# A PSUM bank that keeps operands: y terms, convolution sums and router scratch move in, the third bank for short results goes

## The chip, the cores and the metric

The kernel runs on one core of one Trainium2 chip. The metric is the device time in microseconds of one execution, as the median of several runs. The engines are named as in the profile: PE (TensorE matmuls), PEld (its weight loads), DVE (VectorE), ACT (ScalarE), POOL (GpSimd) and SP (SyncE, which issues most DMAs).

## The reference

Input `x` is 8 images of 256 channels by 32 x 32 pixels, float32. Three layers follow each other, each with a residual. Cut to what matters:

```python
# layer 0: deformable attention on group-normalised x (4 groups = heads of 64 channels)
q   = gconv1x1(x, wq)                                   # 1024 queries per image
off = tanh(pw(gelu(depthwise_conv6x6_stride4(q)))) * 4  # 64 sample places per group
kv  = grid_sample(x, grid + off); k, v = gconv1x1(kv, wk), gconv1x1(kv, wv)
pos = grid_q - grid_kv                                  # 1024 x 64 pairs, x and y
bias = sign(pos) * log1p(abs(pos))
bias = relu(bias @ w1.T + b1)                           # 2 -> 64
bias = relu(bias @ w2.T + b2)                           # 64 -> 64
bias = bias @ w3.T + b3                                 # 64 -> 1
x = x + wo(softmax(q*scale @ k.T + bias) @ v)
# layer 1: tokens t (1024 x 256 per image), n = layernorm(t)
t = t + sigmoid((n @ qw) @ n.T) @ n
# layer 2: mixture of experts, 8 experts, the best 2 per token, n = layernorm(t)
t = t + n + sum over the 2 experts of weight * (gelu(n @ w1[e] + b1[e]) @ w2[e] + b2[e])
```

The position bias of layer 0 is the bulk of the work: 8 x 4 x 1024 x 64 pairs go through a small network of widths 2, 64, 64 and 1.

## The kernel before, in words

**Turns.** The position network sets the beat. An image (a "batch", `b`) takes 128 steps in 64 turns of two steps; the loop over `n` at the end of `tile_conv_attn_hybrid` writes out one turn after the other, and the order in which instructions are written is the order on each engine (`in_order` fixes it). The first layer of a step is separable: a term `ta` that depends on x and a term `nb` that depends on y. An even step computes `ta - nb` on POOL (L465) and ACT rectifies it (L470). An odd step, the "second form", computes `max(ta, nb)` on DVE (L463), and what that leaves out is put right by a term `nc` that `second` gets from `nb` by a small matmul `cp` (L446, copied by ACT in L451). The second layer is the matmul group `h2p` (L478) on PE into one of two tiles of two banks, which ACT empties for even steps (L484) and DVE for odd ones (L486). The third layer is `sim` (L505), every second turn. First-layer results are made two turns ahead (four steps in flight, six buffers).

**Tables.** Every eight turns `terms` loads the next `ta` and `nb`; `scale` (turn 3 of 8) scales them on ACT and DVE (L440), `second` (turn 4 of 8) makes `nc`, and from turn 6 the new table is in use.

**What is laid between the turns.** Each turn takes one step of several generators: `prep` for the next image (group norm, queries, the 36 taps of the convolution on DVE in L284 and L286, three a turn, Gelu, sampling weights, `tp` transposes in L374, `kv`, `kp`), `softmax` (transposes `lt` and `at_`, product `ov`), `attention` of the image before (`upper` and `rest`, with `slots`, `finish` and then `route`), `experts` of an older image (`yp` L921, `hp` L939, `tp` L957), and `combine` (POOL gathers in L992, DVE sums in L984, `op` in L975).

**PSUM.** There are eight banks: one for `sim`, four for `h2p`, two that rotate for short results (`psum(name)`), and one more (`acc(name)`). `aside(name)` takes the bank of `acc`, except while `attending` is set, when it takes one of the two rotating ones:

```python
    def aside(name):
        return psum(name) if attending else acc(name)
```

In `slots`, step `n` makes the scores `ap` of one slot (L713), ACT takes the sigmoid `sg` (L718), and PE adds the product of the slot before to `vp` (L727). `vp` lies in `acc`'s bank and collects all slots of a quarter `q` of the queries (two or four), and then DVE adds it to `x1` (L733). `route` takes `acc`'s bank for the transposed router scores and as scratch for DVE. The convolution's sums `oc` lie in SBUF. The flag `attending` also steers how the last image's experts are laid in.

Of the kernel before, what the change touches and what calls it, by code (L numbers as in the profile page):

```python
# [16 lines left out]
P = 128  # L17
# [5 lines left out]
E = 8  # L23
# [80 lines left out]
def tile_conv_attn_hybrid(ctx: ExitStack, tc: tile.TileContext, x, par, qw, w1, w2_, cst, out):  # L104
# [6 lines left out]
    t8 = ctx.enter_context(tc.tile_pool(name="t8", bufs=7))  # L111
    t2 = ctx.enter_context(tc.tile_pool(name="t2", bufs=11))
    hpool = ctx.enter_context(tc.tile_pool(name="h", bufs=1))
# [20 lines left out]

    def acc(name):
        return ps_a.tile([P, 512], F32, tag="acc", name=name)


    attending = sorting = False

    def aside(name):
        return psum(name) if attending else acc(name)

# [93 lines left out]
    def prep(b, xb, st):  # L237
# [3 lines left out]
        for k in range(2):  # L241
# [3 lines left out]
            yield  # L245
        gm = aside("gm")
        nc.tensor.matmul(gm[:, 0:2], lhsT=cst_("gavg"), rhs=mv[:, :, 0], start=True, stop=True)
# [6 lines left out]
        yield  # L254
        gv = aside("gv")
        nc.tensor.matmul(gv[:, 0:2], lhsT=cst_("gavg"), rhs=dm, start=True, stop=True)
# [12 lines left out]
        for k in range(2):  # L269
            for h in range(2):  # L270
                qs = (aside if h else psum)("qs")
                nc.tensor.matmul(qs, lhsT=wq[:, k, :], rhs=xn[:, k, halves(h)], start=True, stop=True)
                nc.scalar.copy(inside(qp, k, h), qs.rearrange("p (r f x) -> p r f x", f=4, x=W))
            yield


        oc = one.tile([P, 16, 8], F32, name="oc")
        dw = par_("dw")
        for t in range(KS * KS):
# [7 lines left out]
            if t % 3 == 2:  # L287
                yield
        nc.scalar.activation(oc, oc, AF.Gelu)
        oa = oc.rearrange("p (y k) x -> p k y x", k=2)  # L290
        yield


        op = aside("op")
        for g in range(2):
# [33 lines left out]

        fp = aside("fp")  # L330
        nc.tensor.transpose(fp[:, 0:128], ft, ident)
# [33 lines left out]
        for t in range(0, 10, 2):  # L365
            if t:
                w2_ = wt[:, t - 2 : t, :]
                nc.gpsimd.tensor_tensor(w2_, w2_, hx.unsqueeze(1).to_broadcast([P, 2, 256]), ALU.mult)
            if t < 8:
                tp = aside("tp")  # L370
# [12 lines left out]
        kv = aside("kv")  # L383
        for k in range(2):
# [13 lines left out]
        yield  # L398
        kp = aside("kp")
        for k in range(2):  # L400
# [23 lines left out]
    def terms(b, k, h, part):  # L424
# [29 lines left out]

        return (ta, nb, nc_, b, number), scale, second

    def first_layer(terms_, n):
        ta, nb, nc_, of, number = terms_
        h1 = hpool.tile([P, 2, 16, W], F32, name="h1", bufs=6)
        a = ta[:, n].unsqueeze(2).to_broadcast([P, 2, 16, W])  # L460
        b = nb[:, n].unsqueeze(3).to_broadcast([P, 2, 16, W])
        if second_form(of, number, n):
            nc.vector.tensor_tensor(h1, a, b, ALU.max)  # L463
            return h1, nc_[:, :, n // 2]
        nc.gpsimd.tensor_tensor(h1, a, b, ALU.subtract)  # L465
        return h1, None
# [127 lines left out]
    def attention(b, st, o, rt):  # L594
        nonlocal attending
        x = xres.pop(b)
# [106 lines left out]
        def slots(todo, last):  # L703
            sg = None
            for n in range(len(todo) + 1):
                sg_, sg = sg, None
                if n < len(todo):
                    q, mp = todo[n]
                    ap = psum("ap").rearrange("p (u i) -> p u i", u=2)
                    for u in range(2):  # L710
                        m0 = (2 * mp + u) * P
                        for k in range(2):
                            nc.tensor.matmul(  # L713
                                ap[:, u, :], lhsT=tn[:, k, m0 : m0 + P], rhs=qt[:, k, quarter(q)],
                                start=(k == 0), stop=(k == 1),
                            )
                    sg = low("sg")
                    nc.scalar.activation(sg, ap, AF.Sigmoid)  # L718
                if sg_ is not None:
                    q, mp = todo[n - 1]  # L720
                    first = n == 1 or todo[n - 2][0] != q
                    end = n == len(todo) or todo[n][0] != q
                    if first:
                        vp = acc("vp").rearrange("p (i c) -> p i c", i=2)
                    for u in range(2):
                        for i in range(2):
                            nc.tensor.matmul(  # L727
                                vp[:, i, :], lhsT=sg_[:, u, i * P : (i + 1) * P], rhs=tt[:, 2 * mp + u, :],
                                start=(first and u == 0 and i == 0), stop=(end and u == 1), skip_group_check=True,
                            )  # L730
                    if end:
                        xs = x1[:, 2 * q : 2 * q + 2, :]
                        nc.vector.tensor_tensor(xs, xs, vp, ALU.add)  # L733
                        if last:
                            finishing.append(finish(q))
                yield
# [55 lines left out]
    def route(lqs, rt, slots_):  # L792
# [5 lines left out]

        revv = rev.unsqueeze(1).to_broadcast([P, 8, E])
        bank = acc("lp")  # L800

        def part(n, size=64):
            a = bank[:, Q + 64 * n : Q + 64 * n + size]
            return a.rearrange("p (m e) -> p m e", e=E) if size == 64 else a

        for c in range(2):
            nc.tensor.transpose(bank[:, c * P : (c + 1) * P], lqs[:, c * P : (c + 1) * P], ident)
# [37 lines left out]
        most = N // slots_  # L845
        need = bank[:, Q + 64 : Q + 64 + 8 * most].rearrange("p (e n) -> p e n", e=E)
        nc.vector.tensor_tensor(
# [8 lines left out]
        nc.vector.tensor_reduce(ends[:, 1:9], part(1), AX.X, ALU.add)  # L856
        for c in range(2):
            nc.vector.tensor_scalar(ws[c], m1, 0.5 - c, 0.5, ALU.mult, ALU.add)
        yield
        at = part(3)  # L860
        nc.vector.scalar_tensor_tensor(
            at, ends[:, 0:8].unsqueeze(1).to_broadcast([P, 8, E]), float(slots_), cnt[:, 0:8, :], ALU.mult, ALU.add
        )
        place = one.tile([P, 2, 8], F32, name="place")
        for c, oh in enumerate((oh1, oh2)):
# [4 lines left out]
        yield  # L870
        which = bank[:, 0 : TILES * (E - 1)].rearrange("p (t e) -> p t e", e=E - 1)
        nc.vector.tensor_tensor(
# [13 lines left out]
    def experts(b, rt):  # L886
# [28 lines left out]
        for n in range(rounds + 2):  # L915
# [107 lines left out]
    total = NB * STEPS  # L1023
    table, scale, second = terms(0, 0, 0, 0)
# [28 lines left out]

# [26 lines left out]
    for n in range(NB * TURNS):  # L1080
# [16 lines left out]
        if coming_ < total and n % 8 == 0:  # L1097
            b_, k_, h_ = place(coming_)
            coming, scale, second = terms(b_, k_, h_, coming_ // 16 % 2)
        if n % 8 == 6 and coming_ < total:  # L1100
# [150 lines left out]
```

## Time and profile before

| | us |
|---|---|
| runs (3): median, lowest, highest | 3148.32, 3146.1, 3148.73 |
| the profiled execution, its own time | 3125.55 |
| its span, first to last instruction | 3123.8 |
| PE busy | 2832.1 (91% of the span) |
| DVE busy | 2170.5 (69%) |
| ACT busy | 1824.4 (58%) |
| POOL busy | 1558.2 (50%) |
| mean granted TensorE clock | 0.975 |

Busy times come from one profiled execution. A group of the profile is a line of the kernel with an engine, an operation and the tiles it writes and reads (`out<-in`); behind the bar stand the busy time in all and the mean of one in ns, and behind the second bar the idle time of the engine just before these instructions with what ended it. Idle time of an engine that nobody waits for costs nothing.

### The profile page before, as it was taken

The numbers are of one execution on the slowest core, as the hardware profiler recorded it, in microseconds if no ns is written. First come the engines' busy times: TensorE is split into PE (matmuls) and PEld (weight loads), VectorE is DVE, ScalarE is ACT, GpSimd is POOL, SyncE is SP. The second block draws the span as 40 slices with busy tenths as digits, with TensorE's granted clock in tenths as the row PEclk, the third lists the DMA queues.
The fourth block names the chain that finished last, engine by engine and source line by source line (L and its number), as shares of the span: only waits on it lengthen the run. The fifth ranks groups of instructions, "written<-read, shape, count | busy, mean of one in ns | idle before, by whom it ended". The sixth has DMA issues, their size and how long they took to land. (4 is left out here: it accounts for less than half of the span.)

```text
span 3123.8 us, 51635 instructions
## 1 busy us (share of the span) xinstructions
PE 2832.1 (91%) x19592; PEld 1395.6 (45%) x19592; DVE 2170.5 (69%) x2999; ACT 1824.4 (58%) x2533; POOL 1558.2 (50%) x945
## 2 busy tenths in 40 slices
PE   3888998899999999999999999899999999979975
PEld 2223343233545344453545445354444545514764
DVE  4897678967776687857876678766877574595122
ACT  3666565665576566665566656665666666554322
POOL 2546454744455364645556455553646443383122
PEclk7999999999999999999999999999999999989998
DMA  3312101211256125531346223561245325631386
GB/s 106 83 32 48 21 14 32 58 38 21 75 139 187 23 63 140 168 107 43 77 111 208 51 57 100 144 179 33 61 132 173 88 78 153 173 97 57 112 280 221
DMA packets 428297, 311.21 MB, mean 100 GB/s; under 512 B 284432, under 2 KB 368656, under 8 KB 428048
## 3 DMA queue, kind: packets, MB, share of 16 engines
q1 hardware_dynamic: 415472, 273.14, 32.7%
q0 software_dynamic: 12288, 33.57, 3.4%
q8 instruction: 154, 2.52, 0.3%
q10 hardware_dynamic: 288, 1.20, 0.1%
q14 instruction: 95, 0.78, 0.1%
HBM read 239.93 MB, written 67.90 MB: 99 GB/s over the span
## 5 line engine op out<-in xcount | busy, mean ns | idle before, releaser
L465 POOL TENSOR_TENSOR h<-ta,nb 128x1024 f32<-128x1024 f32 x512 | 1071.6, 2095 | 1036.2 <-PE h2p L478 913.1
L478 PE MATMUL h2p<-h,pr__100 64*64 64x512 f32 x8192 | 1028.3, 610 | 131.8 <-DVE h L486 107.5
L486 DVE TENSOR_TENSOR h<-h2p,nc 128x1024 f32<-128x1024 f32 x512 | 624.6, 1220 | 461.4 <-PE h2p L478 454.7
L484 ACT ACTIVATE h<-h2p,pr__100 128x1024 f32<-128x1024 f32 x512 | 570.9, 1115 | 517.0 <-PE h2p L478 515.8
L463 DVE TENSOR_TENSOR h<-ta,nb 128x1024 f32<-128x1024 f32 x512 | 769.2, 1503 | 0.3
L470 ACT ACTIVATE h<-h 128x1024 f32<-128x1024 f32 x512 | 538.0, 1051 | 63.4 <-POOL h L465 63.2
L478 PEld LDWEIGHTS h2p<-h,pr__100 64*64 64x64 f32 x8192 | 253.7, 133 | 658.0 <-issue 295.1
L505 PE MATMUL sim<-h,pr__100 128*32 128x512 f32 x4096 | 511.5, 618 | 0.0
L505 PEld LDWEIGHTS sim<-h,pr__100 128*32 128x32 f32 x4096 | 109.5, 112 | 377.8 <-issue 377.8
L713 PE MATMUL ap<-qt,tn 128*128 128x256 f32 x1024 | 250.5, 388 | 0.5 <-ACT nc L451 0.5
L727 PE MATMUL vp<-tt,sg 128*128 128x256 f32 x1024 | 243.3, 381 | 0.3 <-ACT sg L718 0.3
L992 POOL DMA_INDIRECT gs<-ys,slot x128 | 139.0, 1086 | 175.3 <-DMA ys<-yt 55.7
L713 PEld LDWEIGHTS ap<-qt,tn 128*128 128x128 f32 x1024 | 185.2, 190 | 88.5 <-issue 55.0
L947 ACT ACTIVATE ht<-hp,w 128x128 f32<-128x128 f32 (+1 forms) x366 | 108.6, 377 | 196.8 <-PE hp L939 173.2
L921 PE MATMUL yp<-w,ht 128*128 128x256 f32 x792 | 196.2, 390 | 13.7 <-DMA w<-in_w 7.0
L727 PEld LDWEIGHTS vp<-tt,sg 128*128 128x128 f32 x1024 | 193.2, 190 | 33.2 <-issue 6.9
L939 PE MATMUL hp<-xg,w 128*128 128x128 f32 (+1 forms) x1464 | 197.0, 287 | 6.7 <-ACT gk L307 2.8
L939 PEld LDWEIGHTS hp<-xg,w 128*128 128x128 f32 x1464 | 187.8, 194 | 18.3 <-ACT gk L307 3.7
L775 POOL DMA_INDIRECT xs<-ut,slot x128 | 167.8, 1311 | 51.0 <-DVE slot L869 29.4
L921 PEld LDWEIGHTS yp<-w,ht 128*128 128x128 f32 x792 | 144.4, 191 | 73.0 <-issue 34.0
L926 DVE TENSOR_TENSOR yt<-yp,w 128x512 f32<-128x512 f32 x99 | 68.3, 690 | 153.5 <-PE yp L921 127.3
L286 DVE SCALAR_TENSOR_TENSOR oc<-qp,pr__100,oc 128x128 f32<-128x128 f32 x280 | 168.9, 603 | 7.2
(266 smaller groups left out, 2468.0 us busy)
## 6 DMA issues: line engine op xcount, KB each, us to landing
w<-in_w SPq DMA_DIRECT2D x183, 384.0 KB, 3.6
w<-in_w SPq DMA_DIRECT2D x183, 257.0 KB, 3.7
ta<-fd SPq DMA_DIRECT2D x128, 256.0 KB, 5.5
xl<-xs SPq DMA_DIRECT2D x99, 256.0 KB, 3.7
ys<-yt SPq DMA_DIRECT2D x99, 256.0 KB, 2.3
nb<-fd SPq DMA_DIRECT2D x128, 128.0 KB, 5.3
xb<-in_x SPq DMA_DIRECT2D x8, 1024.0 KB, 7.2
x<-in_x SPq DMA_DIRECT2D x8, 1024.0 KB
```

The lines of the kernel that those rows point to most:

```text
L286: nc.vector.scalar_tensor_tensor(oc, tap, dw[:, t : t + 1], oc, ALU.mult, ALU.add)
L463: nc.vector.tensor_tensor(h1, a, b, ALU.max)
L465: nc.gpsimd.tensor_tensor(h1, a, b, ALU.subtract)
L470: nc.scalar.activation(h1, h1, AF.Relu)
L478: nc.tensor.matmul(h2p[gs, r, :], lhsT=par_("w2")[rs, gs], rhs=h1[rs, g].rearrange("p y x -> p (y x)"), start=True, stop=True, tile_positi ...
L484: nc.scalar.activation(h2, h2p, AF.Relu, bias=par_("cb2"))
L486: nc.vector.tensor_tensor(h2.rearrange("p r (y x) -> p r y x", x=W), h2p.rearrange("p r (y x) -> p r y x", x=W), nc_.unsqueeze(3).to_broad ...
L505: nc.tensor.matmul(sim[32 * q : 32 * q + 32, :], lhsT=par_("z3")[:, 15 - m : 47 - m], rhs=h2s[2 * u + q // 2][:, q % 2, :], start=False, s ...
L713: nc.tensor.matmul(ap[:, u, :], lhsT=tn[:, k, m0 : m0 + P], rhs=qt[:, k, quarter(q)], start=(k == 0), stop=(k == 1),)
L727: nc.tensor.matmul(vp[:, i, :], lhsT=sg_[:, u, i * P : (i + 1) * P], rhs=tt[:, 2 * mp + u, :], start=(first and u == 0 and i == 0), stop=( ...
L921: nc.tensor.matmul(yp[:, s, :], lhsT=ht[:, f, s * P : (s + 1) * P], rhs=f2[:, s * several // 2, f * C : (f + 1) * C], start=(f == 0), stop ...
L939: nc.tensor.matmul(hp[:, f, us], lhsT=f1[:, u, k * C + f * P : k * C + (f + 1) * P], rhs=xg[:, k, us], start=(k == 0), stop=(k == 1),)
```

## The change

One bank, the one that `acc` gave out, is allocated once as `still` and never rotates. Its first half, `held_nb`, holds the y terms of the eight second-form steps of the table in use; ACT copies them there in two halves (`hold(0)` behind `second`, `hold(1)` two turns later), and L463 reads its y operand from there in place of SBUF. Its other half, `shared`, holds the convolution's sums `oc` (Gelu then writes a new SBUF tile `oa`), and `route`'s scratch. All other users of `acc` and `aside` take the two rotating banks. In `slots`, `vp` sums two slots in a row, in one rotating bank, every second step, and `x1` gets its sum after each pair. The pool `t2` has 12 buffers in place of 11. In `route`, the line that reads the counts moves ahead of a `yield`. The first image's `kv` takes a tile of `h2p`.

```diff
-    t2 = ctx.enter_context(tc.tile_pool(name="t2", bufs=11))
+    t2 = ctx.enter_context(tc.tile_pool(name="t2", bufs=12))
...
-    def acc(name):
-        return ps_a.tile([P, 512], F32, tag="acc", name=name)
-    attending = sorting = False
-    def aside(name):
-        return psum(name) if attending else acc(name)
+    still = ps_a.tile([P, 512], F32, tag="still", name="still")
+    held_nb = still[:, 0:256].rearrange("p (s g y) -> p s g y", g=2, y=16)
+    shared = still[:, 256:512]
+    attending = sorting = convolving = False
...
-        gm = aside("gm")
+        gm = psum("gm")
...
-                qs = (aside if h else psum)("qs")
+                qs = psum("qs")
...
-        oc = one.tile([P, 16, 8], F32, name="oc")
+        nonlocal convolving
+        convolving = True
+        oc = shared[:, 0:128].rearrange("p (y x) -> p y x", x=8)
...
-        nc.scalar.activation(oc, oc, AF.Gelu)
-        oa = oc.rearrange("p (y k) x -> p k y x", k=2)
+        oa = one.tile([P, 2, 8, 8], F32, name="oa")
+        nc.scalar.activation(oa.rearrange("p k y x -> p y k x"), oc.rearrange("p (y k) x -> p y k x", k=2), AF.Gelu)
+        convolving = False
...
-        kv = aside("kv")
+        kv = psum("kv") if b else ps_h.tile([P, 2, 512], F32, tag="h2p", name="h2p")[:, 0, :]
...
-        kp = aside("kp")
+        kp = psum("kp")
...
+        def hold(half):
+            nc.scalar.copy(held_nb[:, 4 * half : 4 * half + 4], nb[:, 8 * half + 1 : 8 * half + 8 : 2])
...
         if second_form(of, number, n):
+            b = held_nb[:, n // 2].unsqueeze(3).to_broadcast([P, 2, 16, W])
             nc.vector.tensor_tensor(h1, a, b, ALU.max)
...
         def slots(todo, last):
-            sg = None
+            sgs = []
             for n in range(len(todo) + 1):
-                sg_, sg = sg, None
                 if n < len(todo):
                     q, mp = todo[n]
                     ap = psum("ap").rearrange("p (u i) -> p u i", u=2)
...
+                if n and n % 2 == 0:
+                    q = todo[n - 1][0]
+                    vp = psum("vp").rearrange("p (i c) -> p i c", i=2)
+                    for s in range(2):
+                        for u in range(2):
+                            for i in range(2):
+                                nc.tensor.matmul(
+                                    vp[:, i, :], lhsT=sgs[s][:, u, i * P : (i + 1) * P],
+                                    rhs=tt[:, 2 * todo[n - 2 + s][1] + u, :],
+                                    start=(s == u == i == 0), stop=(s == u == 1), skip_group_check=True,
+                                )
+                    sgs.clear()
+                if n < len(todo):
                     sg = low("sg")
                     nc.scalar.activation(sg, ap, AF.Sigmoid)
-                if sg_ is not None:
-                    q, mp = todo[n - 1]
-                    first = n == 1 or todo[n - 2][0] != q
-                    end = n == len(todo) or todo[n][0] != q
-                    if first:
-                        vp = acc("vp").rearrange("p (i c) -> p i c", i=2)
-                    for u in range(2):
-                        for i in range(2):
-                            nc.tensor.matmul(
-                                vp[:, i, :], lhsT=sg_[:, u, i * P : (i + 1) * P], rhs=tt[:, 2 * mp + u, :],
-                                start=(first and u == 0 and i == 0), stop=(end and u == 1), skip_group_check=True,
-                            )
-                    if end:
-                        xs = x1[:, 2 * q : 2 * q + 2, :]
-                        nc.vector.tensor_tensor(xs, xs, vp, ALU.add)
-                        if last:
-                            finishing.append(finish(q))
+                    sgs.append(sg)
+                if n and n % 2 == 0:
+                    xs = x1[:, 2 * q : 2 * q + 2, :]
+                    nc.vector.tensor_tensor(xs, xs, vp, ALU.add)
+                    if last and (n == len(todo) or todo[n][0] != q):
+                        finishing.append(finish(q))
                 yield
...
-        bank = acc("lp")
         def part(n, size=64):
-            a = bank[:, Q + 64 * n : Q + 64 * n + size]
+            a = shared[:, 64 * n : 64 * n + size]
...
+        bank = psum("lp")
...
-        for c in range(2):
-            nc.vector.tensor_scalar(ws[c], m1, 0.5 - c, 0.5, ALU.mult, ALU.add)
-        yield
         at = part(3)
         nc.vector.scalar_tensor_tensor(
             at, ends[:, 0:8].unsqueeze(1).to_broadcast([P, 8, E]), float(slots_), cnt[:, 0:8, :], ALU.mult, ALU.add
         )
+        yield
+        for c in range(2):
+            nc.vector.tensor_scalar(ws[c], m1, 0.5 - c, 0.5, ALU.mult, ALU.add)
...
-                tp = aside("tp").rearrange("p (k i) -> p k i", k=2)
+                tp = psum("tp").rearrange("p (k i) -> p k i", k=2)
...
     scale()
     second()
+    for half in range(2):
+        hold(half)
...
-            return softmax(sts[b], k, h, ss, os_[b], aside)
+            return softmax(sts[b], k, h, ss, os_[b], psum)
...
             elif n % 8 == 4:
                 second()
+                hold(0)
+            elif n % 8 == 6:
+                hold(1)
```

More of the change, by code (lines that the diff above doesn't have):

```diff
@@ L254, in prep @@
         yield
-        gv = aside("gv")
+        gv = psum("gv")
         nc.tensor.matmul(gv[:, 0:2], lhsT=cst_("gavg"), rhs=dm, start=True, stop=True)
@@ L288, in prep @@
                 yield
-        nc.scalar.activation(oc, oc, AF.Gelu)
-        oa = oc.rearrange("p (y k) x -> p k y x", k=2)
+        oa = one.tile([P, 2, 8, 8], F32, name="oa")
+        nc.scalar.activation(oa.rearrange("p k y x -> p y k x"), oc.rearrange("p (y k) x -> p y k x", k=2), AF.Gelu)
+        convolving = False
         yield
-        op = aside("op")
+        op = psum("op")
         for g in range(2):
@@ L328, in prep @@
         yield
-        fp = aside("fp")
+        fp = psum("fp")
         nc.tensor.transpose(fp[:, 0:128], ft, ident)
@@ L369, in prep @@
             if t < 8:
-                tp = aside("tp")
+                tp = psum("tp")
                 tpv = tp.rearrange("p (t k c) -> p t k c", k=2, c=P)
@@ L453, in second @@
                 )
-        return (ta, nb, nc_, b, number), scale, second
+        def hold(half):
+            nc.scalar.copy(held_nb[:, 4 * half : 4 * half + 4], nb[:, 8 * half + 1 : 8 * half + 8 : 2])
+        return (ta, nb, nc_, b, number), scale, second, hold
     def first_layer(terms_, n):
@@ L594, in attention @@
     def attention(b, st, o, rt):
-        nonlocal attending
         x = xres.pop(b)
@@ L799, in route @@
         revv = rev.unsqueeze(1).to_broadcast([P, 8, E])
-        bank = acc("lp")
+        assert not convolving
         def part(n, size=64):
-            a = bank[:, Q + 64 * n : Q + 64 * n + size]
+            a = shared[:, 64 * n : 64 * n + size]
             return a.rearrange("p (m e) -> p m e", e=E) if size == 64 else a
+        bank = psum("lp")
         for c in range(2):
@@ L845, in route @@
         most = N // slots_
-        need = bank[:, Q + 64 : Q + 64 + 8 * most].rearrange("p (e n) -> p e n", e=E)
+        need = shared[:, 64 : 64 + 8 * most].rearrange("p (e n) -> p e n", e=E)
         nc.vector.tensor_tensor(
@@ L870, in route @@
         yield
-        which = bank[:, 0 : TILES * (E - 1)].rearrange("p (t e) -> p t e", e=E - 1)
+        which = shared[:, 0 : TILES * (E - 1)].rearrange("p (t e) -> p t e", e=E - 1)
         nc.vector.tensor_tensor(
@@ L1023, in tile_conv_attn_hybrid @@
     total = NB * STEPS
-    table, scale, second = terms(0, 0, 0, 0)
+    table, scale, second, hold = terms(0, 0, 0, 0)
     while "sampled" not in sts[0]:
@@ L1098, in tile_conv_attn_hybrid @@
             b_, k_, h_ = place(coming_)
-            coming, scale, second = terms(b_, k_, h_, coming_ // 16 % 2)
+            coming, scale, second, hold = terms(b_, k_, h_, coming_ // 16 % 2)
         if n % 8 == 6 and coming_ < total:
```

## The prediction

> **What bounds the kernel now.** I read the page's busy times first, then the costliest groups, then the list of waits, and last the order of time around single stalls. The first line of the page gives the engine to watch:
>
> ```profile
> PE 2832.1 (91%) x19592; PEld 1395.6 (45%) x19592; DVE 2170.5 (69%) x2999; ACT 1824.4 (58%) x2533; POOL 1558.2 (50%) x945
> ```
>
> PE is idle for 3123.8 - 2832.1 = 291.7 us only, so whatever the change does must pass through that idle time or add to it. Busy time by stage (columns: stretch, its length, then PE, PEld, DVE, ACT, POOL) tells where it lies:
>
> ```profile
> 100.00:330.00 230.00, 197.53 (x1497) 57.95 (x1489) 195.32 (x229) 146.84 (x177) 126.42 (x61) 0.96 0.20 44
> 870.00:2690.00 1820.00, 1729.68 (x12273) 876.20 (x12271) 1309.66 (x1798) 1140.63 (x1610) 953.04 (x576) 1.00 0.41 111
> ```
>
> In the first batch DVE (195 of 230 us) is as loaded as PE; in the long middle, five batches of 363 us, PE is 95% busy and 90 us idle in all. The groups that the change touches, and PE's waits in front of h2p:
>
> ```profile
> L465 POOL TENSOR_TENSOR h<-ta,nb 128x1024 f32<-128x1024 f32 x512 | 1071.6, 2095 | 1036.2 <-PE h2p L478 913.1
> L478 PE MATMUL h2p<-h,pr__100 64*64 64x512 f32 x8192 | 1028.3, 610 | 131.8 <-DVE h L486 107.5
> L486 DVE TENSOR_TENSOR h<-h2p,nc 128x1024 f32<-128x1024 f32 x512 | 624.6, 1220 | 461.4 <-PE h2p L478 454.7
> ...
> L463 DVE TENSOR_TENSOR h<-ta,nb 128x1024 f32<-128x1024 f32 x512 | 769.2, 1503 | 0.3
> ...
> L286 DVE SCALAR_TENSOR_TENSOR oc<-qp,pr__100,oc 128x128 f32<-128x128 f32 x280 | 168.9, 603 | 7.2
> ```
>
> L463 and L486 have the same shape; L463 reads two SBUF tensors, L486 one PSUM tensor and one SBUF tensor. L486 lies between 1.21 and 1.23 us in all 512 rows; L463 has a median of 1.218 us, but 116 rows run to 1.4 to 4.1 us. The order of time shows what stretches them:
>
> ```profile
> 1502.79 0.97 POOL L992 DMA_INDIRECT gs<-ys,slot  x1 [0.16 <-issue]
> ...
> 1503.33 3.46 DVE L463 TENSOR_TENSOR h<-ta,nb 128x1024 f32<-128x1024 f32 x1
> ...
> 1503.78 1.92 POOL L465 TENSOR_TENSOR h<-ta,nb 128x1024 f32<-128x1024 f32 x1
> ...
> 1505.86 1.77 POOL L992 DMA_INDIRECT gs<-ys,slot  x1 [0.16 <-issue]
> ```
>
> L463 stands from 1503.33 to 1506.79: two POOL rows pass, POOL's L465 ends at 1505.70, and 1.09 us later L463 is done. The next gather (0.97 us before) takes 1.77 and ends after L463. The two engines shut each other out.
>
> **DVE gets rid of the lock.** With the y terms in PSUM, L463 has L486's operand kinds; I take 1.22 us (bounds 1.22 and today's 1.50). That frees 512 x 0.283 = 145 us of DVE. L286 becomes PSUM plus SBUF; its unlocked rows have a median of 0.446 us, L284 with the same tap takes 0.395, and L866, which reads and writes PSUM, is within 0.01 us of the SBUF-only L829 (0.232 and 0.224); I keep 0.446: 280 x 0.157 = 44 us. These 189 us count only where PE waited. So I walked through DVE's rows in time, gave a credit for each L463 row above 1.218 and L286 row above 0.446, set it to zero whenever DVE stood idle for over 0.1 us, and let each PE wait that DVE ended use up credit. Example: L463 of 2.63 us at 1245.91 gives 1.41, and 1.41 of the 1.97 us that PE waits until 1249.72 goes. In all: 17 us before 400 us, 10 to 870, 22 to 2690, 4 after: **-53**. Many waits stay: 0.44 us before h2p in turns where L486 starts at once and is simply longer than the h2p pair that covers it, and waits behind L440, L872 and L984, which stay locked. Bounds 0 and -107.5 (all of PE's waits for L486).
>
> POOL's L465 falls from 2.095 to about 1.92 us (90 us of POOL), but POOL waits for PE (913 us). It reaches PE only through ACT's L470 and L484, where PE waits 22.7 us: I take **-5** (0 to -22.7).
>
> The Trainium skill (SBUF — State Buffer, Who interferes with whom) says that DVE with two SBUF inputs and a GpSimd instruction that reads SBUF exclude each other, and that whoever starts first holds the port. The first half fits L463 against L486. The second does not fit the rows above, where L463 is shown starting 0.45 us ahead of L465 and still ends after it; by that half L465, not L463, would have been stretched there. By the first half alone the gain would be the same 53. The sum goes by the rows.
>
> **Short results get two banks where there were three.** Until now `acc` took the vp sums, lp, and outside attention also tp, lt, ov, kv and others, beside two rotating banks. Now all rotate over two, so each waits for the reader of the one two before it. No row shows that order, but before's rows give it: start of each PE group less end of the last reader of the group two earlier. The plainest place:
>
> ```profile
> 1232.54 0.66 PE L546 MATMUL lt<-cs,ss 128*128 128x128 f32 x4
> ...
> 1233.13 1.06 PE L686 MATMUL lq<-un,pr__100 128*32 128x256 f32 x8
> ...
> 1234.12 1.99 PE L921 MATMUL yp<-w,ht 128*128 128x256 f32 x8
> ...
> 1234.76 0.88 DVE L537 TENSOR_TENSOR ex<-lt,mx 128x128 f32<-128x128 f32 x4
> ```
>
> yp would take lt's bank, which DVE reads until 1235.64: PE stops for 1.52 us. A batch of the middle has nine such places: yp after lt 1.52; vp, tp and at_ right after cp (which takes both banks) 3 x 0.55; hp after prep's tp 0.48; hp after lt 1.48, of which 0.75 is a locked L463 that goes; tp after yp 1.10, and 1.44 of which 1.27 goes; hp after ov 1.70. Together 7.4 us, x 5 = 37; the first three batches have 4 and the last one, with attention alone, some 7: **+48**. High end: 82, the whole trace without any relief; low end 15, if the places that DVE empties (5.2 of the 7.4) vanish with a faster DVE. What still hides most uses is the h2p pair (1.95 us) and sim (1.92 us) between them.
>
> **Copies into the bank.** hold adds 128 ACT copies of 128x128; L451 (PSUM to SBUF, same size) has 0.365 us, so 47 us on an engine 58% busy: no cost by themselves. But the bank is one tensor, so ACT's copy, DVE's L463, the convolution and route's scratch follow each other in program order. After `second` the copy ends about 1.5 us after cp starts (cp at 1291.14, L451 done at 1292.27, plus 0.37); until then DVE's taps and the next L463 wait, and behind them that turn's evictions. In the middle PE has 3 us and more of other work and L463's result is needed two turns later: hidden. In the first two batches (16 tables, turns of 4.3 us) I count 0.4 to 0.6 us each, and 0.6 in each route: **+10** (0 to 64 x 1.6 = 100, if nothing hides it). By the skill (PSUM — Partial Sum Buffer, PSUM bank collisions raise a hardware error) two engines may not touch one bank and quadrant at once even at different columns, so the halves can't be used independently. That speaks against the change; no row of before has ACT and DVE share a bank in this way, and without this order the +10 would be 0.
>
> **Pairs in attention.** The number of vp matmuls stays. x1's adds rise from 48 to 64: 16 x 0.686 = 11 us on DVE, in its idle time. Turns become uneven: every second one loses 1.89 us of PE work that the next gets. L463, L486 and three taps are 3.8 us of DVE against a short turn of 1.95 + 1.89 us; in attention (1110 to 1245 us) L486 now ends a median of 3.4 us before PE needs its bank, so little shows: **+6** (0 to 8 batches x 8 turns x 1 us). Two copies stand before the first turn (2 x 0.365): **+1** (0 to 3). route's moved lines, the twelfth t2 buffer and Gelu's new output (0.31 us, 8 times) I put at nothing; ACT's and DVE's idle time covers them, and uncovered they are under 3 us.
>
> **Sum:** -53 - 5 + 48 + 10 + 6 + 1 = +7 us. The profiled execution took 3125.55 us (span 3123.8 and 1.75 around it), 22.8 under the median of the runs, 3148.32; the +7 applied to the median gives 3155. Its own range, with the terms half way to their bounds, is 3135 to 3180.
>
> **Rivals.** (1) Faster: DVE and ACT, freed of locks, empty the banks in time. Banks cost 20, holds and pairs nothing, POOL gives 15: -48, 3100. For it: 5.2 of 7.4 us per batch hang on DVE. Against: ov's 1.70 stems from L413's lock, which stays, and lt's 1.52 has no lock in it. It holds once the costs fall below 58 us. (2) Slower: the holds couple ACT, DVE and PE. If after each `second` PE's second h2p comes back before taps and L463 are through, 64 tables lose 0.8 us: 51 in place of 10, so 3196. DVE's margin is the start of the second h2p group less the end of the L486 one turn earlier. For this rival: the margin is 0.06 us, a bare signal's time, in half the turns before 330 us; against it: 1.1 us or more in three quarters of the middle's turns. It decides where DVE's margin is below 1 us. (3) The lock does not go: gain 0, +65, 3213; L486's 512 even rows speak against it.
>
> **How the numbers follow.** Forecast 0.47 (0.08 of it below -0.2%, 0.15 within, 0.24 above), (1) 0.27, (2) 0.20, (3) 0.04, other mishaps 0.02. 0.2% is 6.3 us, about what a measurement of this kernel can tell from no change. Faster 0.35, same 0.15, slower 0.50. The range 3100 to 3205 takes in (1) and (2).
>
> **What would show it.** L463 at 1.22 with no row above 1.3, L286 at 0.45; PE's wait for L486 before h2p near 55 us; new waits before yp, hp, tp and at_ of 40 us or more behind DVE L537, L563, L926 and ACT L451. If those stay under 20 us, (1) is right; if L463 stands idle behind ACT's copy for 50 us and PE's wait for L486 does not fall, (2).

## The result, and the profile after

The changed kernel takes 3126.21 us (median of 4 runs, 3122.98 to 3131.93) against 3148.53 (4 runs, 3146.1 to 3149.97) for the kernel before: ratio 0.9932, 95% interval 0.9913 to 0.995. It is 21 us faster, where the prediction had +7 us. The time lies in the range of the prediction; the sign was the other one.

The profiled execution of the changed kernel took 3122.98 us (span 3121.2). The spans of the two profiles shown lie 2.6 us apart only, because the profiled execution of before was a quick one. A second profile of before (span 3148.6 us) has 9.4 us more of PE's busy time and 11 us more in the last image's experts. So the profiles are compared here stage by stage, and times by the runs.

The first line of the page after:

```profile
PE 2830.1 (91%) x19592; PEld 1395.6 (45%) x19592; DVE 1979.1 (63%) x3015; ACT 1849.0 (59%) x2661; POOL 1377.1 (44%) x945
```

DVE lost 191 us of busy time and POOL 181; ACT gained 25. Idle time of PE is the same in sum (291.7 and 291.1 us; 307.1 in the second profile of before), so the stages have to be looked at one by one. Here is busy time by stage, for the first two batches of before (from the first h2p turn of a batch to that of the next):

```profile
70.80:345.20 274.40, 238.53 (x1782) 73.14 (x1781) 227.36 (x264) 175.18 (x206) 152.62 (x72) 0.96 0.24 60
345.20:680.70 335.50, 301.83 (x2102) 125.35 (x2101) 265.26 (x345) 200.85 (x250) 182.47 (x101) 0.98 0.16 36
```

and of after, then the fixed window of the middle that the prediction showed:

```profile
72.50:328.50 256.00, 231.39 (x1782) 72.36 (x1781) 203.70 (x264) 177.88 (x221) 129.60 (x71) 0.99 0.25 63
328.50:648.70 320.20, 298.92 (x2104) 124.32 (x2103) 232.34 (x347) 203.78 (x266) 155.12 (x101) 0.98 0.17 37
...
870.00:2690.00 1820.00, 1723.90 (x12170) 871.78 (x12166) 1175.10 (x1765) 1144.93 (x1674) 837.63 (x571) 0.99 0.40 110
```

The first two batches are 18.4 and 15.3 us shorter, 34 us in all. The same 1782 matmuls of the first batch keep PE busy 7.1 us less, at a clock of 0.99 in place of 0.96. In the middle PE does less in the same 1820 us (12170 matmuls where 12273 were): a batch there takes 366 us, some 3 us more than in the quick profile of before, whose tables of groups stand in the prediction, and about what its second profile has there (364 to 368). The groups after:

```profile
L484 PE MATMUL h2p<-h,pr__101 64*64 64x512 f32 x8192 | 1027.9, 610 | 97.6 <-DVE h L492 71.1 <-ACT h L490 20.9 <-issue 4.2
L471 POOL TENSOR_TENSOR h<-ta,nb 128x1024 f32<-128x1024 f32 x512 | 980.4, 1916 | 1154.9 <-PE h2p L484 991.8 <-ACT xg L966 68.3 <-issue 36.0
L492 DVE TENSOR_TENSOR h<-h2p,nc 128x1024 f32<-128x1024 f32 x512 | 625.4, 1222 | 462.3 <-PE h2p L484 455.0
L469 DVE TENSOR_TENSOR h<-ta,still 128x1024 f32<-128x1024 f32 x512 | 620.5, 1212 | 47.4 <-ACT still L458 45.4 <-ACT oa L291 0.8
L287 DVE SCALAR_TENSOR_TENSOR still<-qp,pr__101,still 128x128 f32<-128x128 f32 x280 | 126.6, 452 | 7.2
...
L458 ACT COPY still<-nb 128x128 f32<-128x128 f32 x128 | 35.2, 275 | 34.0 <-DVE h L469 33.7
```

L469 (L463 before) is down to 1.212 us, with none of its 512 rows above 1.3, L287 (L286) to 0.452, and L471 (L465) to 1.916. The lock between these two is gone: in the order of time after, L469 beside a POOL instruction keeps its length, and POOL's 2.00 us stay near their mean of 1.916:

```profile
1504.51 2.00 POOL L471 TENSOR_TENSOR h<-ta,nb 128x1024 f32<-128x1024 f32 x1 [1.54 <-PE h2p L484]
1504.65 1.22 DVE L469 TENSOR_TENSOR h<-ta,still 128x1024 f32<-128x1024 f32 x1
```

PE's wait for DVE in front of h2p fell from 107.5 to 71.1 us, and the new waits for banks are these (list of waits; us in total, times, longest):

```profile
PE hp L946 <- DVE o L569: 7.9, 5, 1.6
...
PE tp L964 <- DVE yt L933: 4.6, 11, 0.6
...
PE hp L946 <- ACT xt L377: 3.7, 10, 0.4
...
PE vp L727 <- ACT nc L453: 3.3, 7, 0.5
...
PE yp L928 <- ACT lqs L696: 2.8, 6, 0.5
```

The place that the prediction called the plainest is not among them. PE's order there, after:

```profile
1199.49 0.66 PE L552 MATMUL lt<-cs,ss 128*128 128x128 f32 x4
1200.08 1.06 PE L691 MATMUL lq<-un,pr__101 128*32 128x256 f32 x8
1201.60 1.99 PE L928 MATMUL yp<-w,ht 128*128 128x256 f32 x8 [0.47 <-ACT lqs L696]
```

yp waits 0.47 us for the reader of lq, not 1.52 us for DVE's reading of lt. In the whole trace no short result waits for lt's reader.

### The profile page after: what moved, and what is told of

Read it like the earlier page. It is cut to its first block, busy times and chain, and to the rows that moved or that the text cites. A ratio compares the mean times of both kernels' runs of the same rounds, so it can differ in the third digit from the quotient of the medians.

```text
span 3121.2 us, 51810 instructions
## 1 busy us (share of the span) xinstructions
PE 2830.1 (91%) x19592; PEld 1395.6 (45%) x19592; DVE 1979.1 (63%) x3015; ACT 1849.0 (59%) x2661; POOL 1377.1 (44%) x945
## 5 line engine op out<-in xcount | busy, mean ns | idle before, releaser
L471 POOL TENSOR_TENSOR h<-ta,nb 128x1024 f32<-128x1024 f32 x512 | 980.4, 1916 | 1154.9 <-PE h2p L484 991.8
L484 PE MATMUL h2p<-h,pr__101 64*64 64x512 f32 x8192 | 1027.9, 610 | 97.6 <-DVE h L492 71.1
L492 DVE TENSOR_TENSOR h<-h2p,nc 128x1024 f32<-128x1024 f32 x512 | 625.4, 1222 | 462.3 <-PE h2p L484 455.0
L469 DVE TENSOR_TENSOR h<-ta,still 128x1024 f32<-128x1024 f32 x512 | 620.5, 1212 | 47.4 <-ACT still L458 45.4
L511 PE MATMUL sim<-h,pr__101 128*32 128x512 f32 x4096 | 498.1, 604 | 0.0
L727 PE MATMUL vp<-tt,sg 128*128 128x256 f32 x1024 | 233.0, 381 | 3.5 <-ACT nc L453 3.3
L999 POOL DMA_INDIRECT gs<-ys,slot x128 | 125.9, 984 | 205.1 <-issue 56.4
L739 DVE TENSOR_TENSOR x<-x,vp 128x512 f32<-128x512 f32 x64 | 44.0, 688 | 244.3 <-PE vp L727 244.3
L735 ACT ACTIVATE sg<-ap 128x512 f32<-128x512 f32 x128 | 76.4, 597 | 151.7 <-PE ap L717 139.6
## 6 DMA issues: line engine op xcount, KB each, us to landing
ta<-fd SPq DMA_DIRECT2D x128, 256.0 KB
xl<-xs SPq DMA_DIRECT2D x99, 256.0 KB
ys<-yt SPq DMA_DIRECT2D x99, 256.0 KB
```

Of the source, the lines that this page charges most:

```text
L484: nc.tensor.matmul(h2p[gs, r, :], lhsT=par_("w2")[rs, gs], rhs=h1[rs, g].rearrange("p y x -> p (y x)"), start=True, stop=True, tile_positi ...
L492: nc.vector.tensor_tensor(h2.rearrange("p r (y x) -> p r y x", x=W), h2p.rearrange("p r (y x) -> p r y x", x=W), nc_.unsqueeze(3).to_broad ...
L511: nc.tensor.matmul(sim[32 * q : 32 * q + 32, :], lhsT=par_("z3")[:, 15 - m : 47 - m], rhs=h2s[2 * u + q // 2][:, q % 2, :], start=False, s ...
L727: nc.tensor.matmul(vp[:, i, :], lhsT=sgs[s][:, u, i * P : (i + 1) * P], rhs=tt[:, 2 * todo[n - 2 + s][1] + u, :], start=(s == u == i == 0) ...
L999: nc.gpsimd.indirect_dma_start(out=got[m][:, c, :], out_offset=None, in_=yv[:, :], in_offset=bass.IndirectOffsetOnAxis(ap=slot[:, c, m : m ...
```

## The experiments

Line numbers are each kernel's own. Differences in microseconds are (ratio - 1) x 3147, 3147 standing for the medians of before that ran beside them (3144.9 to 3148.5).

**The size of an effect that can be told.** Both kernels once more, unchanged. The kernel before:

> The kernel before, unchanged, to see where the 23 us lie between its profiled execution (3125.55) and its other runs (3146 to 3150). Theory A (a stretch in which SP issues one instruction per 0.7 us, as the changed kernel's profile shows from 2976 to 2994 us, comes and goes): turns of all eight batches take what the first profile shows (274, 336, 358, 364, 362, 365, 362 and 374 us), and the difference lies in the last 255 us, behind the last h2p. Theory B (the first profile was a quick execution throughout): every batch is longer by 2 to 3 us.

Ratio 0.9996 (0.9987 to 1.0006). Neither theory holds whole: of the 25 us between its two profiles 11 lie behind the last h2p turn, and the rest in five of the eight batches. The changed kernel:

> The changed kernel, unchanged. Theory A: batches as in its first profile (256, 320, 361, 367, 365, 367, 367, 367), and the part behind the last h2p between 255 (no slow SP stretch) and 276 us (one); the ratio to before again near 0.993. Theory B: batches differ by 2 us or more each from the first profile.

3124.11 us, ratio 0.993 (0.9915 to 0.9945). The gain stands; of its batches one is 4 us longer than in the first profile, the others agree within 1.2 us. Differences under some 4 us are not to be read.

**Two banks without the y terms and the sums in the third.** Of the changed kernel, `oc` returns to SBUF, and L469 reads `nb` from SBUF with no `hold`:

```diff
-            b = held_nb[:, n // 2].unsqueeze(3).to_broadcast([P, 2, 16, W])
...
-                hold(0)
-            elif n % 8 == 6:
-                hold(1)
...
-        oc = shared[:, 0:128].rearrange("p (y x) -> p y x", x=8)
+        oc = one.tile([P, 16, 8], F32, name="oc")
```

> The changed kernel without its gain: L463 reads its y terms from SBUF as before, no copies into the bank, the convolution's sums in SBUF; short results rotate over two banks, pairs in attention and route's scratch as changed. Theory A (the locks give 53 us, the lost third bank takes about 48 and pairs 6): 40 to 60 us slower than before, 3 to 9 us in each middle batch. Rival B (the lost bank costs next to nothing, and the gain is the locks less the copies): within 10 us of before.

3186.08 us, ratio 1.0126 (1.0109 to 1.0143): +40 us. A middle batch has PE idle 21.6 to 23.5 us, against 16.9 to 19.9 in the quick profile of before.

**The y terms alone.** The changed kernel with `oc` in SBUF again:

> The changed kernel with the convolution's sums back in SBUF: only the y terms (and route's scratch) lie in the kept bank. Theory A (L463's locks are three quarters of the gain, and the convolution's taps need not wait for the copies any more): 5 to 15 us slower than the changed kernel, most of it in the first two batches. Rival B (the taps' waits for the copies cost as much as their locks): equal to the changed kernel within 4 us.

3135.89 us, ratio 0.997 (0.9962 to 0.9979): 49 us faster than the kernel just above, 12 us slower than the changed kernel. Of the 12, 7.7 lie in the first batch (263.7 us against 256.0), as Theory A had it.

**The sums alone.** The changed kernel with L469's y operand from SBUF and no `hold`, and with `oc` in PSUM:

> The changed kernel without the y terms: L463 reads SBUF as before and nothing is copied into the bank; the convolution's sums lie in it, with route's scratch. Theory A (the taps' gain, 44 us of DVE, counts in the first two batches alone): 5 to 15 us faster than banks_only, so about 1.009 of before. Rival B (the taps gain only together with the y terms): within 4 us of banks_only.

3182.22 us, ratio 1.0105 (1.0086 to 1.0123): 7 us faster than without the sums in PSUM. The two intervals overlap, so this is the least certain of the differences.

**The pairs alone.** The kernel before, `acc` and all, with `vp` summing two slots at a time in `acc`'s bank, and the twelfth `t2` buffer:

```diff
-    t2 = ctx.enter_context(tc.tile_pool(name="t2", bufs=11))
+    t2 = ctx.enter_context(tc.tile_pool(name="t2", bufs=12))
...
+                if n and n % 2 == 0:
+                    q = todo[n - 1][0]
+                    vp = acc("vp").rearrange("p (i c) -> p i c", i=2)
```

> The kernel before with one part of the change: vp sums two slots at a time, still in the third bank, with an add of x1 per pair (and the twelfth t2 buffer). Theory A (uneven turns cost little): 0 to 8 us slower than before, so that 33 to 41 of the 41 us of banks_only belong to the lost third bank. Rival B (pairs are a good part of that cost): 15 us or more slower.

3140.94 us, ratio 0.9974 (0.9964 to 0.9985): 8 us faster than before, not slower. PE's list of waits gives the likely cause: `at` waits 12.1 us for DVE's `ex` in the second profile of before and 3.8 with the pairs. One place of the kernel before, from that second profile:

```profile
1418.53 0.60 PE L546 MATMUL lt<-cs,ss 128*128 128x128 f32 x4
1419.06 1.95 PE L478 MATMUL h2p<-h,pr__100 64*64 64x512 f32 x16
1420.94 1.99 PE L727 MATMUL vp<-tt,sg 128*128 128x256 f32 x8
...
1430.34 0.55 PE L546 MATMUL at__11683<-cs,ex 128*128 128x128 f32 x3
1432.01 0.33 PE L546 MATMUL at__11683<-cs,ex 128*128 128x128 f32 x1 [1.12 <-DVE ex L537]
```

and the same place with the pairs:

```profile
1409.58 0.60 PE L546 MATMUL lt<-cs,ss 128*128 128x128 f32 x4
1410.11 1.95 PE L478 MATMUL h2p<-h,pr__100 64*64 64x512 f32 x16
1411.99 3.72 PE L722 MATMUL vp<-tt,sg 128*128 128x256 f32 x16
...
1422.33 0.66 PE L546 MATMUL at__11695<-cs,ex 128*128 128x128 f32 x4
```

at needs the softmax that starts from lt. Here vp gives PE 3.72 us of work between the two in place of 1.99, and the 1.12 us in front of at are gone. The uneven turns, for which the prediction gave +6, don't show: PE's wait for DVE's eviction in front of h2p went from 111.1 to 102.5 us, of which 4.0 come back in front of h2p as a wait for DVE's `gmean`. The twelfth `t2` buffer was not taken apart from the pairs.

**The pairs undone in the changed kernel.** `vp` is made and added slot by slot, each time in a rotating bank:

```diff
-                if n and n % 2 == 0:
+                if n:
```

> The changed kernel with vp per slot in place of per pair: every slot sums into its own rotating bank and DVE adds it to x1, 128 adds in place of 64. Theory A (PE has no wait for the adds, and DVE has idle time): within 5 us of the changed kernel, DVE 44 us busier. Rival B (each short result more in the two banks costs PE a wait of 0.2 us or more): 10 us or more slower.

3126.8 us, ratio 0.9931 (0.9915 to 0.9946), the same as with pairs. at waits for ex 3.3 us here too, but vp now waits 10.2 us for ACT's `un`, a wait that the changed kernel does not have. So in the changed kernel the pairs neither gain nor lose; what they gain seems tied to the order of before.

**The holds moved, earlier.** `hold(0)` ahead of `second`:

```diff
             elif n % 8 == 4:
-                second()
                 hold(0)
+                second()
```

> The changed kernel with hold(0) written ahead of second instead of behind it, so that ACT's first copy no longer stands behind PE's cp and the two copies of nc. Theory A (DVE's L469 waits 45 us for ACT's copy in the profile, nearly all of it covered by PE's own work): at most 4 us faster than the changed kernel, while that wait of L469 falls below 25 us. Rival B (the copies couple the engines and cost about the 10 us of the prediction or more): 8 us or more faster, mostly in the first two batches.

3141.8 us, ratio 0.998 (0.9971 to 0.9989): 16 us slower than the changed kernel, and neither theory had that. The order of time shows the chain:

```profile
1130.00 0.45 PE L448 MATMUL cp<-nb,pr__101 64*64 64x128 f32 x8
1130.41 1.21 DVE L469 TENSOR_TENSOR h<-ta,still 128x1024 f32<-128x1024 f32 x1
...
1131.66 0.27 ACT L458 COPY still<-nb 128x128 f32<-128x128 f32 x1 [2.12 <-DVE h L469]
1131.86 0.62 ACT L453 ACTIVATE nc<-cp,ncb 128x128 f32<-128x128 f32 x2
...
1132.28 0.66 PE L552 MATMUL at__9071<-cs,ex 128*128 128x128 f32 x4 [1.83 <-ACT nc L453]
```

ACT's copy waits 2.12 us for DVE's L469 (one bank), and behind it on ACT stand the two copies of cp, which hold both rotating banks. at's wait for ACT's nc is 24.3 us in all in place of 9.0. These 15.3 us are nearly all of the 16.

**The holds moved, later.** One turn later each, away from `second`:

```diff
-                hold(0)
-            elif n % 8 == 6:
+            elif n % 8 == 5:
+                hold(0)
+            elif n % 8 == 7:
                 hold(1)
```

> The changed kernel with hold(0) one turn after second and hold(1) three turns after it. Theory A (the holds are covered where they stand now; what cost 16 us when hold(0) stood ahead of second was the wait of at for the copies of cp): within 4 us of the changed kernel; at still waits 9 us for ACT nc, and DVE's wait for ACT's copy changes without changing PE's wait before h2p by more than 4 us. Theory B (the holds cost the 10 us that I gave them, because hold(0) queues behind the two copies of cp): 6 to 12 us faster than the changed kernel, PE's wait for L492 before h2p down by as much.

3128.03 us, ratio 0.9939 (0.9926 to 0.9953): within 4 us of the changed kernel, as Theory A had it. DVE's L469 waits 8.0 us for ACT's copy in place of 44.7 to 45.4, and PE's wait for DVE in front of h2p stays (72.7 us). So those 45 us, which look like a cost in the table of groups, are covered.

**Gaps made on purpose.** L469 is issued five times in 12 turns:

```diff
-            nc.vector.tensor_tensor(h1, a, b, ALU.max)
+            for _ in range(times):
+                nc.vector.tensor_tensor(h1, a, b, ALU.max)
...
-            new = [first_layer(table, (2 * n + 4 + r) % 16) for r in range(2)]
+            new = [first_layer(table, (2 * n + 4 + r) % 16, 5 if b > 1 and i in (17, 41) else 1) for r in range(2)]
```

> The changed kernel with L469 issued five times in place of once in 12 turns (two in each of the last six batches): 4 x 1.21 = 4.8 us more on DVE in each. Theory A (a gap of PE costs twice: the gap itself, and a stretch at half clock some 10 us later): PE waits 1.5 to 3.5 us at each place, half of the 12 are followed by a half-clock stretch of 3.4 us or more, so half-clock time rises by 20 us or more, PE's busy time for the same instructions by 10 us or more, and the time by 30 to 50 us over the changed kernel (about 3155 to 3175). Theory B (the clock has nothing to do with PE's gaps): the time rises by the gaps alone, 18 to 40 us, and PE's busy time stays within 3 us.

3187.87 us, ratio 1.0129 (1.0114 to 1.0145): 63 us more than the changed kernel, above what either theory gave. Theory A's second price is there: against the second profile of the changed kernel PE is idle 47 us more, and it is busy 17 us more (2846.6 against 2829.6) for the same 19592 matmuls; half-clock stretches from 870 to 2690 us add up to 64.9 us in place of 22.1. One place:

```profile
1868.48 6.23 DVE L470 TENSOR_TENSOR h<-ta,still 128x1024 f32<-128x1024 f32 x5
...
1869.50 1.09 PE L485 MATMUL h2p<-h,pr__101 64*64 64x512 f32 x8
...
1875.90 1.99 PE L485 MATMUL h2p<-h,pr__101 64*64 64x512 f32 x8 [5.31 <-DVE h L493]
1877.82 1.71 PE L504 MATMUL sim<-qp,kd 128*128 128x512 f32 x2
```

DVE's extra 4.8 us pass to PE in full (PE stands for 5.31 us), because the eviction L493 is queued behind them. The eight matmuls behind the gap take 1.99 us where eight of the same shape took 1.09 ahead of it. The half clock does not come some 10 us after the gap, as Theory A said: here its step begins at 1875.59 us, as the gap ends. The gaps cost more than I gave them also in another place: tp's wait for DVE's `yt`, which is queued behind the same repeats, is 28.8 us, where the two profiles of the changed kernel have 4.6 and 10.4.

**Two DVE operations to ACT.** The eviction of ov and the scaling of c (L415):

```diff
-            nc.vector.tensor_scalar(ch, ch, lin[:, 0, f : f + 1], lin[:, 1, f : f + 1], ALU.mult, ALU.add)
+            nc.scalar.activation(ch, ch, AF.Identity, bias=lin[:, 1, f : f + 1], scale=lin[:, 0, f : f + 1])
...
-        nc.vector.tensor_copy(o[:, k, halves(h)], ov)
+        nc.scalar.copy(o[:, k, halves(h)], ov)
```

> The changed kernel with two DVE operations moved to ACT: the eviction of ov into o (32 times 0.68 us) and the scaling of c (L415, 32 times 0.66 us). Theory A (waits of two banks are plain costs, and each that goes is time): hp's wait for o, 7.9 us, goes, and DVE has 43 us less; 6 to 14 us faster than the changed kernel. Theory B (the place only changes its name: hp then waits for ACT's eviction, or ACT's longer queue delays L490 and the holds): within 4 us of it.

3111.02 us, ratio 0.9884 (0.9869 to 0.9899): 15 us faster than the changed kernel and the fastest of all. hp's wait for o, 7.9 us, is now one of 1.0 us:

```profile
PE hp L946 <- ACT o L569: 1.0, 5, 0.2
```

About 7 us more lie in the first batch (252.7 us, in the changed kernel 256.0) and the last (363.3 and 366.9 us). Which of the two operations gave them was not separated.

**Both.** Later holds and the two operations on ACT together:

> Both edits of the two kernels before in one: the later holds, and ov's eviction and c's scaling on ACT. Theory A (the gains add, as the terms touch other waits): the sum of the two differences within 4 us. Theory B (ACT is the queue they share: the later holds meet the moved evictions): 5 us or more slower than the better of the two alone.

3114.53 us, ratio 0.9899 (0.9884 to 0.9914). That is 10 us faster than the changed kernel; the two differences add up to 12. Theory A holds, and nothing is gained over the kernel above.

## Why the prediction was wrong

Kernels from above make a chain from before to after, in which the second step holds all that is left of the change (two banks, route's scratch and moved lines, Gelu's new output, the first image's `kv`) and the others one edit each:

| step | measured, us | predicted, us |
|---|---|---|
| pairs | -8 | +6 |
| two banks in place of three, route's scratch and the rest | +48 | +48 |
| sums in PSUM | -7 | |
| y terms in PSUM, with the holds | -54 | |
| the last two together | -61 | -53 - 5 + 10 + 1 = -47 |
| sum | -21 | +7 |

(+48 is +40 with the pairs less the pairs' own -8. By the other order of edits the y terms bring 49 and the sums 12.)

Two steps of the prediction failed. The pairs, +6 in its sum, gained 8. And the term for the locks, -53, counted the idle time of PE alone and put the slower matmuls behind a gap at nothing: from the kernel with two banks to the changed one PE is idle 44 us less (334.9 to 291.1), near the -47 of the sum for locks, POOL and copies, but also busy 20 us less (2850.6 to 2830.1). These are single profiles, and the two of before lie 9.4 us apart in PE's busy time.

**Banks: the sum was right, the places only in part.** Some places came as worked out: hp after ov waits 1.58 us (predicted 1.70), vp, tp and at after cp 0.5 each (0.55; one such wait of at in each middle batch stood there before the change, and now there are two). The two places behind lt did not come. I had followed yp's bank to lt, and the trace shows that it waits for lq's reader. Between the kernel with the pairs alone and the one with two banks, PE's idle time in a middle batch grew by 3 to 6 us, not by 7.4, and its busy time, for which the sum had no term, by 2 to 4 us. The second made up for the first, and about 10 of the 48 us lie where the sum had no place, behind the last h2p turn (277.2 us, with the pairs alone 267.4). That +48 came out is luck in part.

**Locks: the lock went as described; the price of a gap had a part missing.** My walk through DVE's rows counted idle time that would go. In the first two batches it gave 17 us up to 400 us and a part of the 10 that follow. Measured there, from the kernel with two banks and nothing else to the changed one, PE is idle 23.5 us less. But it is also busy 9 us less for the same matmuls (539.5 to 530.3 us). This is the clock: half-clock steps take up 33.8 us of these two batches with two banks and 14.5 in the changed kernel, and half of the 19.3 between them is 9.7. In the kernel before, a gap and what comes after it:

```profile
111.48 1.09 PE L478 MATMUL h2p<-h,pr__100 64*64 64x512 f32 x8 [0.44 <-ACT h L484]
114.64 1.99 PE L478 MATMUL h2p<-h,pr__100 64*64 64x512 f32 x8 [2.07 <-DVE h L486]
116.56 2.40 PE L505 MATMUL sim<-h,pr__100 128*32 128x512 f32 x16
...
127.39 1.92 PE L505 MATMUL sim<-h,pr__100 128*32 128x512 f32 x16
```

and the granted clock there (the number behind POOL's):

```profile
114.15:117.56 3.41, 2.92 (x16) 0.65 (x20) 3.41 (x5) 1.30 (x2) 1.07 (x1) 0.50 0.00 0
117.56:120.98 3.42, 2.95 (x27) 1.06 (x20) 2.06 (x2) 0.64 (x3) 0.00 (x0) 1.00 0.00 0
```

After the 2.07 us that PE waits for DVE, eight matmuls take 1.99 in place of 1.09 us, and the sim group 2.40 in place of 1.92: 1.4 us more on top of the 2.07. The prediction showed the clock column (0.96 in the first batch) and put no term on it. The kernel with gaps made on purpose shows that the waits are the cause and the clock the consequence: 47 us of idle time brought 17 us of slower matmuls, 0.36 us for each. With that factor the 53 would have been an estimated 72.

The Trainium skill (TensorE: Matmul & The Clock Gate, HAM oscillation) gives as the rule that PE should have no idle gaps above about 3.4 us. By that rule 83 of the 85 waits for DVE in front of h2p in before, 2.5 us long and less, would have cost nothing beyond themselves; the rows above differ, and they decide.

The prediction also took one row as speaking against "whoever starts first": L463 starts 0.45 us ahead of L465 and is still the one that is stretched. In that row the gather L992 had started 0.54 us ahead of L463. Over the trace of before, 104 of the 116 long rows of L463 start behind an L465 that is still running, and in the other 12 another POOL instruction (L992 or L368) had started ahead of L463, with L465 next behind it. Where L463 starts ahead of L465 and keeps its 1.22 us (119 rows), L465 takes a median of 2.45 us, against 1.91 where the two don't overlap. So the start does decide here. Of POOL's -5 the list shows 2: PE's wait for ACT's h went from 22.7 to 20.9 us.

**Holds: +10 does not show.** L469 does stand behind ACT's copy for 45 us, near the mark that I set for the second rival, but PE's wait for DVE fell all the same, and moving the holds away from `second` takes 37 us of that wait out without any gain. No run has the y terms in the bank without holds, so their price is not shown to be zero. The rival that the holds couple the engines became true only in the kernel that puts hold(0) ahead of the copies of cp, and there through at, not through h2p.

**Pairs: the sign was wrong.** The prediction looked for whom the uneven turns would hurt and did not ask whom the extra vp work would cover. The 1.12 us in front of at stood in the list of waits of before.

**The first rival** had the right side by another way: "Banks cost 20" is not so (48), and its relief of 68 (53, and 15 from POOL) is near the 61 measured, of which a third is the clock that it did not have. Its test, waits behind the evictions under 20 us, gave no clear answer: the list after has some 40 us of new waits for banks, while some 17 us of old ones (at for ex, kp for at, lp for ft) are gone.

**Against the predicted signs:** L469 at 1.212 us without a long row and L287 at 0.452 came as given. PE's wait for L492 in front of h2p is 71, not 55. The new waits stand behind DVE o, DVE yt and ACT nc as named, not behind ex. That the profiled execution of before was some 23 us quicker than the median was told but not explained; half of it is a stretch in the tail (last section), which the second profile of before and both of after have.

## What to carry to other kernels

A wait of the bounding engine has two prices where its clock follows its activity: count the waits that an edit takes away, and then the slower instructions behind those that are long enough, from the profile's own rows. When work is moved, look in the list of waits for what it will cover at its new place as well as for what it will uncover. An idle time behind another engine's copy (45 us of L469's here) says nothing about the end until the copy has been moved and the bounding engine's own waits compared.

## What the runs showed of the hardware that was not expected

**Half clock after less than 2.9 us of idle time.** The granted clock has steps of 3.41 us. In the second profile of before, 20 half-clock stretches lie between 72 and 2760 us, 16 of one step and 4 of two. Each follows directly on a step in which PE was idle for 1.93 us or more in all; in 19 of the 20 this idle time was less than 2.9 us. The other way round, of the steps at full clock all 11 with 2.0 us or more of idle time were followed by half clock, 9 of the 16 with 1.5 to 2.0 us, and none of the 736 with less. In the 14 profiles of this case together these are 126 of 126, 55 of 237 and 1 of 10436. The slow matmuls lie in the half-clock step itself: in the kernel before PE is idle for 2.02 us of the step that ends at 114.15 us, and the step from 114.15 to 117.56 has the clock at 0.50 and the eight matmuls that take 1.99 us. So here a wait costs twice when the idle time of its step comes to about 2 us, and a shorter one costs itself alone.

**A slow stretch of DMA issues.** In the last image's experts SP issues at times four DMAs in 9 to 10 us where it takes 4 us otherwise. The order of time on SP, in the changed kernel and in the quick profile of before (four issues of weights):

```profile
2974.87 9.08 SPq L914 DMA_DIRECT2D w<-in_w  x4
```

```profile
2971.37 3.78 SPq L907 DMA_DIRECT2D w<-in_w  x4
```

The second profile of before has 9.86 us for such a group. PE waits there, and the stretch behind the last h2p turn is 254.9 us in the quick profile, 266.2 in the second profile of before, and 275.6 and 272.4 in the two of after. What starts it was not found. Without a second profile of before all of it would have passed for a cost of the change. Whether a part is one stays open: all eleven profiles with two banks have 272 to 277 us behind the last h2p turn, the three with three banks 255 to 267, but with the y terms in PSUM the batch ahead of it is shorter (368.7 us, before 375.1).
